# Attention with its projections in a block's first step, and a new order of the work behind it

## The chip, the cores and the metric

The kernel runs on one core of a Trainium2 chip. The metric is the device time of one execution in microseconds (us). Engines are named as in the profile: PE (TensorE, matmuls), ACT (ScalarE), DVE (VectorE), POOL (GpSimd) and SP (the queue that issues DMAs).

## The reference

Four layers follow one another on an fp32 tensor of 16 x 384 x 16 x 16 (two clips of 8 frames, 2048 tokens a clip):

```python
# layer 0: attention over all tokens of a clip, 12 heads of 32
qk = (xt @ qk_w.T).reshape(B, N, 2, nh, HEAD_DIM)
...
attn = softmax(einsum('bhnd,bhmd->bhnm', q * scale, k), axis=-1)
attn = alpha * eye + beta * attn - gamma * Cm          # Cm = 1/N everywhere
out = einsum('bhnm,bhmd->bhnd', attn, v)               # v is x itself
# layer 1: depthwise 7x7, LayerNorm, MLP 384->1536->384 with GELU and GRN, + residual
# layer 2: Sobel x and y, 768->384 fusion, LayerNorm, GELU, + residual
# layer 3: BN, 1x1, depthwise 3x3, BN, 1x1, + residual; linear attention over 8 heads, 1x1;
#          LayerNorm, MLP 384->1536->384 with GELU, + residual
```

With `alpha`, `beta` and `gamma` each a number per head, the result of layer 0 is `alpha * x + beta * softmax(qk) x - gamma * mean(x)`: the means over a clip's tokens enter as a bias.

## The kernel before

**Attention.** A *unit* is one clip `b` and one group `g` of four heads (128 channels): 6 units. A unit has 4 *blocks* `n` of 512 queries, and a block has 16 *steps* `t` of 128 keys, so there are 24 blocks and 384 steps. In a step `scores` (L465) does the four heads' score matmuls into two PSUM tiles `st` and two exponentials on ACT into `e`; `weighted` (L483) does the four heads' matmuls of values into the accumulator `av`, and DVE adds the exponentials into `s`. The main loop (L596 to L606) calls `scores` of a step, then `weighted` of the step before, so `weighted` lags one step behind. `av` and `dn` (the denominators) have one PSUM bank each; `st` has three tiles of two banks.

The exponentials' sums become denominators by a matmul with ones (`weights`, L526). `ADDS` (L56) says for each block how many steps DVE sums before such a matmul: with 16, one matmul group at the block's end; with 8, two; with 4, four. Groups inside a block are cut into four parts of 128 queries and spread over later steps.

At a block's last step (L517 to L524) ACT copies `av` to `va` and makes `xg = alpha * x + gm`, where `gm` holds the means; two steps later `finish` copies the denominators to `r` (ACT), and step by step follow a logarithm and an exponential of its negative on ACT (`log`, `invert`: the reciprocal) and four DVE operations (`defect`, `refine`, `scale`, `put`). `due` is the list of such deferred pieces, by step number.

Queries and keys of the next blocks are projected in pairs (`project`, L578) into one `st` tile: 6 matmuls of 128x128x512, each in two passes, and then two ACT copies. This happens in step `SLOT` = 5 of a block (L603), in all blocks up to the first two of the last unit. A key's projection also issues the load of its 512 values by SP. The clip means (L574 to L577) are DVE reductions for the first clip, in steps 0 to 12, and for the second clip 12 ACT accumulations of a chunk each and a closing DVE pair, in every second step from 156 on.

**Filling.** `fill` (L1505), called after each step, gives DVE's spare time to the next layer: the depthwise 7x7 of layer 1 (`conv`, 48 multiply-adds a channel chunk) from step `FIRST` on, and the first layer-1 blocks up to their MLP (`leads`) from step `LEAD` = 326. How much is spare comes from `pace` (L196): an estimate of PE's and DVE's time for each step.

**Later work.** After attention, `plan.all` (L1584) orders the operations of all remaining tasks by a list scheduler: among the operations that could start within `SLACK` of the earliest it takes that of the lowest rank. Ranks per task are in `RANK` (L46): `mid` (layer 2 and most of layer 3), `l1` (layer 1), `l3c` (the last MLP), `conv`. The two MLPs of 8 image blocks run in the groups of `TURNS` (L36), as weights are loaded for a group. The order is fixed when the kernel is built: each engine keeps program order (`InOrder`, L88).

Of the kernel before, what the change touches and what calls it, by code (L numbers as in the profile page):

```python
# [9 lines left out]
F32 = mybir.dt.float32  # L10
# [5 lines left out]
P = 128  # L16
# [12 lines left out]
NBLK = N // BLK  # L29
NIP = NBLK  # L30
NQC = N // P
SLOT = 5
LEAD = 20 * NQC + 6
FIRST = NQC + 10

TURNS = (  # L36
    (0, ((0, 0), (0, 1), (0, 2), (0, 3),)),
# [6 lines left out]
AFTER = ('x4', 0, 2)  # L44

RANK = {  # L46
    "mid": ((7.3, 48.9, 70.4, 82.6), (148.1, 31.6, -5.4, 26.9)),
    "l1": ((125.5, 116.9, 31.6, 62.9), (92.4, 221.3, 38.4, 14.0)),
    "l3c": ((153.2, 335.5, -64.8, 29.8), (10.7, 30.4, 62.7, 79.9)),
    "conv": 470.9,  # L50
}
SLACK = 0.1944
LOGEXP = "natural_log_exp_and_others"
JUNK = 2

ADDS = (16, 16, 16, 16, 8, 16, 8, 4, 4, 16, 16, 16, 8, 8, 4, 8, 16, 16, 8, 8, 4, 8, 4, 4)  # L56
XB, YB, SB = 12, 4, 23
NLEAD = 2
TB = BLK // P
RB = 2 * HW  # L60
HD3 = 48
MOST, LEAST, TINY = 1e18, 1e-11, 1e-19
# [133 lines left out]
def pace(t):  # L196


    n, i = divmod(t - 1, NQC)
    adds = ADDS[n]  # L200
    pe, dve = 2.066, 2.275 if t and i % adds else 0.0
    at = i - adds - 1
    parts = sum(j * adds // 4 == at % adds for j in range(4)) if at >= 0 else 0
    if parts:
        pe += 0.22 * parts
    elif i == 1 and n > 0:
        pe += 0.87
    else:
        pe += 0.09
    if n > 0:  # L210
        dve += {5: 0.66, 6: 0.66, 7: 0.6, 8: 0.66}.get(i, 0.0)
    return pe, dve


# [185 lines left out]
def attention(tc, X, xt, L0, block, small, col, cols, ones, load_qk, banks, fill, bound, tiny):  # L400
# [6 lines left out]
    with ExitStack() as actx:  # L407
# [45 lines left out]
            return made, early, late  # L453


        due = {}

        def unit(u, made, gm):

# [23 lines left out]
            def weighted(n, t, es):  # L483
                if t == 0:
                    acc["av"] = pacc.tile([P, BLK], F32, tag="av", name=f"av_{u}_{n}")
                for h in range(4):
                    pe.matmul(
                        acc["av"][HD * h : HD * (h + 1), :],
                        v[t // TB][:, (t % TB) * P + HD * h : (t % TB) * P + HD * (h + 1)],
                        es[h // 2][:, h % 2, :],  # L490
                        start=(t == 0),
                        stop=(t == NQC - 1),
                    )
                at = t % adds[n]
                for i in range(2):
                    if at == 0:
                        sums[i] = es[i]
                    elif at == 1:
                        s = sp.tile([P, 2, BLK], F32, tag="s", name=f"s_{u}_{n}_{t}_{i}")
                        dve.tensor_tensor(s, sums[i], es[i], ALU.add)  # L500
                        sums[i] = s
                    else:
                        dve.tensor_tensor(sums[i], sums[i], es[i], ALU.add)


                k = (u * NBLK + n) * NQC + t
                if at == adds[n] - 1:
                    parts = 1 if t == NQC - 1 else 4
                    for i in range(parts):
                        due.setdefault(k + 2 + i * adds[n] // 4, []).append(  # L510
                            lambda i=i, summed=dict(sums): weights(
                                n, t, summed, ts(i, BLK // parts)
                            )
                        )
                for f in due.pop(k, ()):
                    f()
                if t == NQC - 1:  # L517
                    va = op.tile([P, BLK], F32, tag="va", name=f"va_{u}_{n}")
                    act.activation(va, acc["av"], AF.Copy, scale=1.0)
                    xg = op.tile([P, BLK], F32, tag="xg", name=f"xg_{u}_{n}")  # L520
                    act.activation(
                        xg, X[b][n][:, g, :], AF.Identity, scale=col("alpha", g), bias=gm
                    )
                    due[k + 2].append(lambda: finish(n, va, xg))  # L524

            def weights(n, t, summed, at):  # L526
                if t == adds[n] - 1 and at.start == 0:
# [7 lines left out]
                        stop=(t == NQC - 1),  # L535
                    )

            def finish(n, va, xg):

                if g == 0:  # L540
                    L0[b][n] = block(f"l0_{b}_{n}")
                k = u * NBLK + n
                r = op.tile([P, BLK], F32, tag="r", name=f"r_{u}_{n}", bufs=1)
                w = op.tile([P, BLK], F32, tag="w", name=f"w_{u}_{n}", bufs=1)
                act.activation(r, acc["dn"], AF.Identity, accum_out=bound[:, 0, k : k + 1])
# [18 lines left out]
                def put():  # L564
                    dve.scalar_tensor_tensor(
                        L0[b][n][:, g, :], va, col("beta", g), xg, ALU.mult, ALU.add
                    )

                for i, f in enumerate([log, invert, defect, refine, scale, put]):
                    due.setdefault((k + 1) * NQC + 3 + i, []).append(f)  # L570

            return scores, weighted

        means = [channel_means(dve, op, X, cols, b, act if b else None) for b in range(NB)]  # L574
        for b, (_, steps) in enumerate(means):
            for i, s in enumerate(steps):
                due[b * NC * NBLK * NQC - 36 * b + (3 - b) * i] = [s]  # L577
        def project(name, steps):  # L578
            pp = bank2(name)
            for copy in [f(pp[:, i, :]) for i, f in enumerate(steps)]:  # L580
                copy()
            return 2.7 * len(steps)

        made, early, late_steps = projections(*units[0])
# [5 lines left out]
        for u, (b, g) in enumerate(units):  # L590
            steps = late_steps
            scores, weighted = unit(u, made, means[b][0][:, g : g + 1])
            if u + 1 < len(units):
                made, early, late_steps = projections(*units[u + 1])
                steps = steps + early
            for n in range(NBLK):  # L596
                for t in range(NQC):
                    es = scores(n, t)
                    added = 0.0
                    if before:  # L600
                        before()
                    before = lambda f=weighted, a=(n, t, es): f(*a)
                    if t == SLOT and steps:  # L603
                        added = project(f"p_{u}_{n}", steps[:2])
                        del steps[:2]
                    fill((u * NBLK + n) * NQC + t, added)  # L606
            assert not steps
        before()
        while due:
            for f in due.pop(min(due)):  # L610
                f()
# [4 lines left out]
def conv_seq_kernel(  # L616
# [391 lines left out]
                yield from extra(f, h)  # L1008
        return hid, made

    def second(hid, first, name, ready, last, before=None):

        po = []
        for f in range(NFC):
# [1 line left out]
            after = [ready[f]] if before is None else [(yield from before(f))]  # L1016
            m = tensor(
                NC * BLK,
                after=after + [("wb", first, k)],
                takes=[("mm", NC)] if f == 0 else [],  # L1020
                gives=[("s", 1)] + ([("wb", 1)] if last and f % NG == NG - 1 else []),
            )
# [13 lines left out]
    def layer1(b, i):  # L1036

        n = f"l1_{b}_{i}"
        at, before, last = turns[b, i, 0]
# [5 lines left out]
        gx = pools["tiny"].tile([P, 2, NFC], F32, tag="gx", name=f"gx_{n}")  # L1045
        squares = []

        def norms(f, h):
# [17 lines left out]
        gs = pools["tiny"].tile([P, 2], F32, tag="gs", name=f"gs_{n}")  # L1066
        dve.tensor_reduce(gs, gx, AX.X, ALU.add)
        m = tensor(120, after=[a], takes=[("mm", 1)])
        yield m
# [4 lines left out]
        gm = pools["tiny"].tile([P, 2], F32, tag="gmean", name=f"gmean_{n}")  # L1074
        dve.tensor_scalar(gm, pg[:, :2], 1.0 / FF, 1e-6, ALU.mult, ALU.add)
        dve.reciprocal(gm, gm)
        for k in range(2):
# [21 lines left out]
                )  # L1099
            return a  # L1100

        po, m = yield from second(hid, at, n, None, last, normed)
# [342 lines left out]
    def layer3c(b, i):  # L1445
# [7 lines left out]
        at, before, last = turns[b, i, 1]  # L1453
        hid, made = yield from hidden(
            d, at, "L3_mlp_b1", n, ds, before, ("hid", b, i, 1), last
        )
        po, m = yield from second(hid, at, n, made, last)
        for c in range(NC):
            a = fused(
                BLK,  # L1460
# [14 lines left out]
    turns, before = {}, None  # L1475
    for at, (k, group) in enumerate(TURNS):
        for b, i in group:
            turns[b, i, k] = (at, before, (b, i) == group[-1])
            before = ("hid", b, i, k)

    bias = Task("bias", 0, fusion_bias())
# [17 lines left out]
    if fast:  # L1499
# [5 lines left out]
        def fill(t, added=0.0):  # L1505
# [3 lines left out]
            if t < 0:  # L1509
                while plan.step(bias):  # L1510
                    pass
                return
            if t % NQC == 10 and t > NQC:
                u, i = divmod(t // NQC - 1, NBLK)
                plan.mark(("l0", u // NC, i, u % NC))
            length, work = pace(t)
# [161 lines left out]
```

## Time and profile before

| | us |
|---|---|
| median of 3 runs | 2658.97 (2658.66 to 2663.05) |
| the profiled execution | 2660.87 |
| its span, first to last instruction | 2659.1 |
| attention, first scores to last denominators | 19.3 to 1030.0 |
| first block, from its first value matmul to the next block's | 24.60 to 66.24 |
| a block with 16 steps a sum (the sixth) | 232.75 to 274.18 |
| a block with 8 (the seventh) | 274.18 to 316.14 |
| a block with 4 (the fifteenth) | 612.60 to 655.38 |
| longest PE gap | 6.54, at 1063.1 |
| PE's last matmul ends | 2652.5 |

All instructions of the program stand under line 98, that of the helper that records them, so groups are told apart by their tiles: `e<-st` is an exponential, `av<-e,v` a value matmul. A timeline line gives the start, the time that a run of equal instructions takes, the engine, the operation, shapes and count, and in brackets the idle time ahead of it with what ended it.

### The profile page before, as it was taken

How to read it: one execution, taken by the hardware profiler on the slowest of the kernel's cores; microseconds unless marked ns; L12 is line 12 of the kernel's file. 1: busy time of each engine (PE TensorE's matmuls, PEld its weight loads, DVE VectorE, ACT ScalarE, POOL GpSimd, SP SyncE). 2: the span in 40 equal slices, each digit the busy share in tenths (PEclk: the TensorE clock that was granted, in tenths of full speed). 3: DMA queues.
4: the chain of work that ended last, by engine and by line, in shares of the span. 5: the costliest groups of instructions: out<-in, count | busy, mean ns of one | idle time of the engine just before them, and what ended most of it. 6: DMA issues, size and time to landing. Idle time of an engine off the chain costs nothing. (4 is left out here: it accounts for less than half of the span.)

```text
span 2659.1 us, 30865 instructions
## 1 busy us (share of the span) xinstructions
PE 2623.8 (99%) x12005; PEld 1035.7 (39%) x12005; DVE 2028.8 (76%) x2604; ACT 1573.3 (59%) x2339; POOL 7.5 (0%) x54
## 2 busy tenths in 40 slices
PE   9999999999999999899999999999999999999999
PEld 2222232223222323344444544444444444445443
DVE  5999999999999989999999999999462140542300
ACT  6888888988888887454636534455246551415311
POOL 0000000000000000000000000000000000000000
PEclk9999999999999999899999999999999999999999
DMA  4000000000000003000001101101210000000000
GB/s 155 1 13 5 5 11 3 13 5 5 9 1 1 13 1 131 0 0 1 0 1 36 36 0 48 37 11 48 71 36 12 24 24 12 13 12 1 0 21 16
DMA packets 29275, 55.56 MB, mean 21 GB/s; under 512 B 1728, under 2 KB 14400, under 8 KB 29120
## 3 DMA queue, kind: packets, MB, share of 16 engines
q1 hardware_dynamic: 29120, 53.51, 6.0%
q8 instruction: 96, 1.57, 0.2%
q14 instruction: 59, 0.48, 0.1%
HBM read 47.21 MB, written 6.29 MB: 20 GB/s over the span
## 5 line engine op out<-in xcount | busy, mean ns | idle before, releaser
L98 ACT ACTIVATE e<-st 128x1024 f32<-128x1024 f32 x768 | 742.1, 1025 | 77.2 <-PE st L98 64.0
L98 DVE TENSOR_TENSOR s<-s,e 128x1024 f32<-128x1024 f32 x568 | 657.5, 1219 | 18.3 <-ACT e L98 17.4
L98 DVE SCALAR_TENSOR_TENSOR y<-l,vec,y 128x420 f32<-128x420 f32 (+8 forms) x1152 | 654.7, 636 | 3.6 <-ACT y L98 0.7
L98 PE MATMUL st<-q,k 32*128 32x512 f32 x3072 | 481.7, 641 | 2.9 <-ACT e L98 1.5
L98 PE MATMUL av<-e,v 128*32 128x512 f32 x3072 | 410.6, 605 | 6.1 <-ACT va L98 3.7
L98 PE MATMUL po_l<-hid_l,wb 128*128 128x512 f32 x576 | 259.7, 600 | 4.0 <-ACT hid_l L98 4.0
L98 PE MATMUL ph_l3c<-d_l3c,wa 128*128 128x512 f32 x576 | 259.1, 594 | 0.0
L98 PE MATMUL ph_l<-y,wa 128*128 128x512 f32 x576 | 258.6, 594 | 0.0
L98 PEld LDWEIGHTS st<-q,k 32*128 32x128 f32 x3072 | 152.0, 183 | 270.6 <-issue 145.7
L98 PE MATMUL po_l3c<-hid_l3c,wb 128*128 128x512 f32 x576 | 253.7, 593 | 0.0
L98 ACT ACTIVATE hid_l3c<-ph_l3c,vec 128x512 f32<-128x512 f32 x96 | 65.8, 687 | 264.8 <-PE ph_l3c L98 264.2
L98 PEld LDWEIGHTS av<-e,v 128*32 128x32 f32 x3072 | 60.6, 108 | 299.9 <-issue 273.0
L98 DVE SCALAR_TENSOR_TENSOR o_l3c<-po_l3c,vec,l 128x512 f32<-128x512 f32 x24 | 17.8, 749 | 197.7 <-PE po_l3c L98 196.6
L98 PEld LDWEIGHTS po_l<-hid_l,wb 128*128 128x128 f32 x576 | 109.4, 192 | 139.7 <-issue 127.6
L98 PEld LDWEIGHTS po_l3c<-hid_l3c,wb 128*128 128x128 f32 x576 | 109.0, 190 | 137.2 <-issue 136.2
L98 PEld LDWEIGHTS ph_l3c<-d_l3c,wa 128*128 128x128 f32 x576 | 108.7, 190 | 137.0 <-issue 130.7
L98 PEld LDWEIGHTS ph_l<-y,wa 128*128 128x128 f32 x576 | 108.5, 190 | 136.2 <-issue 126.1
L98 ACT ACTIVATE hid_l<-ph_l,vec 128x512 f32<-128x512 f32 x96 | 65.8, 686 | 135.1 <-PE ph_l L98 134.8
L98 DVE TENSOR_TENSOR s<-e,e 128x1024 f32<-128x1024 f32 x100 | 117.8, 1220 | 30.7 <-ACT e L98 26.1
L98 PE MATMUL p<-x,wqk_sb 128*128 128x512 f32 x288 | 131.8, 608 | 4.1 <-DMA x<-in_x_dram 4.1
L98 DVE SCALAR_TENSOR_TENSOR g_l3a<-h_l3a,dw,g_l3a 128x450 f32<-128x450 f32 (+1 forms) x192 | 119.2, 699 | 14.9 <-ACT g_l3a L98 14.7
L98 ACT ACT_TABLE_LOAD x88 | 112.9, 1283 | 16.7 <-PE ph_l L98 9.4
(153 smaller groups left out, 2285.8 us busy)
## 6 DMA issues: line engine op xcount, KB each, us to landing
wa<-in_w_dram SPq DMA_DIRECT2D x9, 768.0 KB, 4.3
wb<-in_w_dram SPq DMA_DIRECT2D x9, 768.0 KB, 4.8
wa<-in_mlp_w_dram SPq DMA_DIRECT2D x9, 768.0 KB, 4.3
wb<-in_mlp_w_dram SPq DMA_DIRECT2D x9, 768.0 KB, 4.4
v<-in_xt_dram SPq DMA_DIRECT2D x24, 256.0 KB, 2.7
out_dram<-o_l3c SPq DMA_DIRECT2D x24, 256.0 KB, 2.0
x<-in_x_dram SPq DMA_DIRECT2D x7, 768.0 KB, 11.0
qkv<-in_qkv_wT_dram SPq DMA_DIRECT2D x3, 576.0 KB, 11.5
```

What stands on the lines that cost most here:

```text
L98: self.last = self.tc.keep_in_program_order(make(*args, **kw))
```

## The change

- Projections move from step 5 to step 0 of a block, behind `scores` of that step and `weighted` of the last step of the block before.
- The copies `va` and `xg` of the block before come in that step too (`finish` now returns them as `copies`), ahead of the projection's matmuls; behind them one chunk of the second clip's means in each of blocks 1 to 12 (two pieces in the last of these).
- The last denominator matmul, `r`, logarithm, inversion and the DVE operations come in steps 1, 1, 2, 3, 4, 5, 6, 7 (before: 1, 1, 3, 4, 5, 6, 7, 8). Parts of denominator matmuls stay within their block.
- `ADDS` changes for three blocks: 3 (16 to 8), 13 (8 to 16), 23 (4 to 16).
- `pace` gets other rates; `FIRST` is one step earlier, as is the step in which a block of layer 0 counts as done (9 instead of 10).
- `RANK` and `SLACK` are new. In the later work a second MLP layer may start only when that of the block before it in its group is planned; three small tiles get 4 buffers instead of 2.

```diff
-SLOT = 5
-FIRST = NQC + 10
+FIRST = NQC + 9
...
-    "mid": ((7.3, 48.9, 70.4, 82.6), (148.1, 31.6, -5.4, 26.9)),
-    "l1": ((125.5, 116.9, 31.6, 62.9), (92.4, 221.3, 38.4, 14.0)),
-    "l3c": ((153.2, 335.5, -64.8, 29.8), (10.7, 30.4, 62.7, 79.9)),
-    "conv": 470.9,
+    "mid": ((-26.8, 59.3, 121.4, 6.1), (-9.9, 89.9, 76.1, -44.6)),
+    "l1": ((99.2, -11.0, 54.4, 108.8), (48.0, 102.3, -47.4, 64.0)),
+    "l3c": ((77.2, 238.7, 72.9, 521.4), (108.5, 22.1, 82.6, 122.3)),
+    "conv": 381.3,
 }
-SLACK = 0.1944
+SLACK = 0.1686
...
-ADDS = (16, 16, 16, 16, 8, 16, 8, 4, 4, 16, 16, 16, 8, 8, 4, 8, 16, 16, 8, 8, 4, 8, 4, 4)
+ADDS = (16, 16, 16, 8, 8, 16, 8, 4, 4, 16, 16, 16, 8, 16, 4, 8, 16, 16, 8, 8, 4, 8, 4, 16)
...
-    pe, dve = 2.066, 2.275 if t and i % adds else 0.0
+    pe, dve = 2.156, ADD if t and i % adds else 0.0
     at = i - adds - 1
-    parts = sum(j * adds // 4 == at % adds for j in range(4)) if at >= 0 else 0
-    if parts:
-        pe += 0.22 * parts
-    elif i == 1 and n > 0:
-        pe += 0.87
-    else:
-        pe += 0.09
+    if at >= 0:
+        pe += 0.22 * sum(j * adds // 4 == at % adds for j in range(4))
+        pe += 0.22 * (adds < 8 and i == NQC - 1)
     if n > 0:
-        dve += {5: 0.66, 6: 0.66, 7: 0.6, 8: 0.66}.get(i, 0.0)
+        pe += 0.87 * (i == 1)
+        dve += {4: 0.66, 5: 0.66, 6: 0.6, 7: 0.66}.get(i, 0.0)
...
-                if at == adds[n] - 1:
-                    parts = 1 if t == NQC - 1 else 4
-                    for i in range(parts):
-                        due.setdefault(k + 2 + i * adds[n] // 4, []).append(
-                            lambda i=i, summed=dict(sums): weights(
-                                n, t, summed, ts(i, BLK // parts)
-                            )
+                if t == NQC - 1:
+                    ends.append(finish(n, dict(sums)))
+                elif at == adds[n] - 1:
+                    for i in range(4):
+                        due.setdefault(min(k + 2 + i * adds[n] // 4, k - t + NQC - 1), []).append(
+                            lambda i=i, summed=dict(sums): weights(n, t, summed, ts(i, P))
                         )
...
-                if t == NQC - 1:
-                    va = op.tile([P, BLK], F32, tag="va", name=f"va_{u}_{n}")
-                    act.activation(va, acc["av"], AF.Copy, scale=1.0)
-                    xg = op.tile([P, BLK], F32, tag="xg", name=f"xg_{u}_{n}")
-                    act.activation(
-                        xg, X[b][n][:, g, :], AF.Identity, scale=col("alpha", g), bias=gm
-                    )
-                    due[k + 2].append(lambda: finish(n, va, xg))
...
-                for i, f in enumerate([log, invert, defect, refine, scale, put]):
-                    due.setdefault((k + 1) * NQC + 3 + i, []).append(f)
+                todo = [sum_up, sums_out, log, invert, defect, refine, scale, put]
+                for i, f in zip((1, 1, 2, 3, 4, 5, 6, 7), todo):
+                    due.setdefault((k + 1) * NQC + i, []).append(f)
+                return copies
...
-        for b, (_, steps) in enumerate(means):
-            for i, s in enumerate(steps):
-                due[b * NC * NBLK * NQC - 36 * b + (3 - b) * i] = [s]
+        for i, s in enumerate(means[0][1]):
+            due[3 * i] = [s]
+        later = list(means[1][1])
...
-                    if t == SLOT and steps:
+                    if t == 0 and ends:
+                        ends.pop()()
+                        for f in later[: 1 + (len(later) == 2)]:
+                            f()
+                            later.remove(f)
+                    if t == 0 and steps:
                         added = project(f"p_{u}_{n}", steps[:2])
                         del steps[:2]
...
-                after=after + [("wb", first, k)],
+                after=after + [("wb", first, k)] + ([turn] if f == 0 and turn else []),
+                makes=done if f == NFC - 1 else None,
...
-            if t % NQC == 10 and t > NQC:
+            if t % NQC == 9 and t > NQC:
```

`project` itself now emits each of its two steps' matmuls and copy in turn:

```diff
-            for copy in [f(pp[:, i, :]) for i, f in enumerate(steps)]:
-                copy()
+            for i, f in enumerate(steps):
+                f(pp[:, i, :])()
```

More of the change, by code (lines that the diff above doesn't have):

```diff
@@ L59 @@
 TB = BLK // P
+ADD = 2.275
 RB = 2 * HW
@@ L453, in projections @@
             return made, early, late
-        due = {}
+        due, ends = {}, []
         def unit(u, made, gm):
@@ L536, in weights, with finish, copies, sum_up @@
                     )
-            def finish(n, va, xg):
-                if g == 0:
-                    L0[b][n] = block(f"l0_{b}_{n}")
+            def finish(n, summed):
                 k = u * NBLK + n
+                va = op.tile([P, BLK], F32, tag="va", name=f"va_{u}_{n}")
+                xg = op.tile([P, BLK], F32, tag="xg", name=f"xg_{u}_{n}")
                 r = op.tile([P, BLK], F32, tag="r", name=f"r_{u}_{n}", bufs=1)
                 w = op.tile([P, BLK], F32, tag="w", name=f"w_{u}_{n}", bufs=1)
-                act.activation(r, acc["dn"], AF.Identity, accum_out=bound[:, 0, k : k + 1])
+                def copies():
+                    act.activation(va, acc["av"], AF.Copy, scale=1.0)
+                    act.activation(
+                        xg, X[b][n][:, g, :], AF.Identity, scale=col("alpha", g), bias=gm
+                    )
+                def sum_up():
+                    weights(n, NQC - 1, summed, ts(0, BLK))
+                def sums_out():
+                    act.activation(
+                        r, acc["dn"], AF.Identity, accum_out=bound[:, 0, k : k + 1]
+                    )
                 def log():
@@ L564, in put @@
                 def put():
+                    if g == 0:
+                        L0[b][n] = block(f"l0_{b}_{n}")
                     dve.scalar_tensor_tensor(
@@ L608, in attention @@
         before()
+        ends.pop()()
         while due:
@@ L1009, in hidden, with second @@
         return hid, made
-    def second(hid, first, name, ready, last, before=None):
+    def second(hid, first, name, ready, last, before=None, turn=None, done=None):
         po = []
@@ L1038, in layer1 @@
         n = f"l1_{b}_{i}"
-        at, before, last = turns[b, i, 0]
+        at, before, former, last = turns[b, i, 0]
         s, a = yield from centred_later(n, b, i)
@@ L1043, in layer1 @@
         ds = yield from affine(y, "L1_ln_g", "L1_ln_b", a)
-        gx = pools["tiny"].tile([P, 2, NFC], F32, tag="gx", name=f"gx_{n}")
+        gx = pools["tiny"].tile([P, 2, NFC], F32, tag="gx", name=f"gx_{n}", bufs=4)
         squares = []
@@ L1065, in layer1 @@
         yield a
-        gs = pools["tiny"].tile([P, 2], F32, tag="gs", name=f"gs_{n}")
+        gs = pools["tiny"].tile([P, 2], F32, tag="gs", name=f"gs_{n}", bufs=4)
         dve.tensor_reduce(gs, gx, AX.X, ALU.add)
@@ L1073, in layer1 @@
         yield ready
-        gm = pools["tiny"].tile([P, 2], F32, tag="gmean", name=f"gmean_{n}")
+        gm = pools["tiny"].tile([P, 2], F32, tag="gmean", name=f"gmean_{n}", bufs=4)
         dve.tensor_scalar(gm, pg[:, :2], 1.0 / FF, 1e-6, ALU.mult, ALU.add)
@@ L1100, in normed @@
             return a
-        po, m = yield from second(hid, at, n, None, last, normed)
+        po, m = yield from second(
+            hid, at, n, None, last, normed, former, ("sec", b, i, 0)
+        )
         for c in range(NC):
@@ L1452, in layer3c @@
         ds = yield from affine(d, "L3_ln_w", "L3_ln_b", a)
-        at, before, last = turns[b, i, 1]
+        at, before, former, last = turns[b, i, 1]
         hid, made = yield from hidden(
@@ L1456, in layer3c @@
         )
-        po, m = yield from second(hid, at, n, made, last)
+        po, m = yield from second(
+            hid, at, n, made, last, None, former, ("sec", b, i, 1)
+        )
         for c in range(NC):
@@ L1477, in conv_seq_kernel @@
         for b, i in group:
-            turns[b, i, k] = (at, before, (b, i) == group[-1])
+            former = None if (b, i) == group[0] else ("sec", *before[1:])
+            turns[b, i, k] = (at, before, former, (b, i) == group[-1])
             before = ("hid", b, i, k)
```

## The prediction

> **What bounds the kernel now.** I read the page first, then the busy time by stretch, then the timelines of a block's edge.
>
> ```profile
> span 2659.1 us, 30865 instructions
> ## 1 busy us (share of the span) xinstructions
> PE 2623.8 (99%) x12005; PEld 1035.7 (39%) x12005; DVE 2028.8 (76%) x2604; ACT 1573.3 (59%) x2339; POOL 7.5 (0%) x54
> ```
>
> PE is busy nearly throughout. The stretches show that this holds in each stage, and who stands close behind (columns: length, then each engine's busy time):
>
> ```profile
> 25.00:1030.00 1005.00, 998.18 (x7415) 292.73 (x7407) 956.97 (x983) 844.42 (x1009) 0.00 (x0) 1.00 0.02 7
> 1030.00:1850.00 820.00, 804.42 (x2277) 368.13 (x2278) 800.39 (x1265) 422.93 (x823) 3.38 (x24) 0.99 0.08 27
> 1850.00:2659.00 809.00, 802.51 (x2267) 367.18 (x2266) 266.29 (x336) 296.35 (x495) 3.38 (x24) 1.00 0.06 21
> ```
>
> DVE follows PE closely in attention (to 1030 us) and in the first half of the later work; the last third is PE's alone. So time comes and goes with PE's gaps, with PE's work, and with stalls inside its "busy" time. In quiet stretches two attention steps take 4.31 us (scores start at 263.98 and 268.29), 2.155 a step, while ACT needs 2 x 0.92 for its exponentials. ACT has 0.3 us a step to spare, and a longer insert reaches PE within a step.
>
> A block's edge, ACT then PE, and below them the first projection of all:
>
> ```profile
> 273.52 0.60 ACT L98 ACTIVATE va<-av 128x512 f32<-128x512 f32 x1
> 274.00 0.82 ACT L98 ACTIVATE xg<-x,gm,vec 128x512 f32<-128x512 f32 x1
> 274.70 3.77 ACT L98 ACTIVATE e<-st 128x1024 f32<-128x1024 f32 x4
> ...
> 290.52 0.59 ACT L98 COPY q<-p 128x512 f32<-128x512 f32 x1 [3.60 <-PE p L98]
> ```
>
> ```profile
> 274.18 1.07 PE L98 MATMUL av<-e,v 128*32 128x512 f32 x8 [0.28 <-ACT va L98]
> 275.17 1.74 PE L98 MATMUL st<-q,k 32*128 32x512 f32 x8
> ...
> 285.07 5.42 PE L98 MATMUL p<-x,wqk_sb 128*128 128x512 f32 x12
> ```
>
> ```profile
> 11.43 0.59 ACT L98 COPY k<-p 128x512 f32<-128x512 f32 x1 [0.48 <-PE p L98]
> ```
>
> Copies va and xg hold ACT 1.18 us (273.52 to 274.70), and PE waits openly and stretches its next scores. The projection keeps PE 5.35 us (285.07 to 290.42); ACT idles 3.60 of it. The third thing to see: the copy of q waits until 290.52, the end of all 12 matmul passes, though q's own six (0.43 apart) end at 287.9. At 11.43 it is the same: ACT had been free since 10.95 and k's matmuls were over at 9.1. The two halves of the projection's PSUM tile are guarded as one.
>
> **The change, part by part.** *The projection's own order.* Before, all 12 passes went out ahead of both copies. Now the first copy is issued between the halves. If the tile is guarded as one for a write after a read too, the second half's matmuls must wait for the first copy: 0.04 us to its start (290.487 to 290.525), 0.59 for it, some 0.10 back to PE: 0.73 us of an idle PE. Where a mean stands on ACT, it is more: ACT gets to the copy at 1.18 (scores to exponential) + 1.84 (two of them) + 1.18 (va, xg) + 0.83 = 5.03 us after the step's scores start, the first half is done at 1.08 + 1.0 + 2.6 = 4.68, so 0.32 more, 1.05. Blocks 1 to 12 have a mean, 13 to 20 none, block 21 projects one half only: 12 x 1.05 + 8 x 0.73 = 18.4 us. If the halves are guarded apart it is nothing. No row shows a write after a read; the nearest rows, the copies' starts, say one guard, so I take +18.4. Behind the waiting matmuls stand the next scores and all of PE; nothing covers it.
>
> *The edge.* A block with 16 steps a sum runs from 232.75 to 274.18 (first value matmuls): 41.43 us. Less 16 x 2.155 = 34.48, the projection 5.35 and the denominators' matmuls 0.87, 0.73 remain for the edge, and this goes under the projection. But the logarithm (0.61, 283.77 to 284.38) and the inversion (0.75 with its accumulator read), today just ahead of and inside ACT's 3.60 idle us, fall into plain steps 3 and 4. The last block, without a projection, shows their price: its step with the logarithm takes 2.44 instead of 2.07, the one with the inversion about 0.15 more; by arithmetic the latter could cost 0.35. So -0.73 + 0.52 to 0.72: -0.1 for each of 9 projecting 16-step blocks. Blocks with 8 steps a sum take 41.96 (274.18 to 316.14); less four partial sums of 0.22 as well, 0.38 remain, so they save 0.38 and pay 0.52 to 0.72: +0.25 for each of 8. Those with 4 take 42.78 (612.60 to 655.38), their 12 partial sums fill the slack, and 0.3 at most can be saved: +0.3 for each of 4. Sum -0.9 + 2.0 + 1.2 = +2.3 us; with both pieces free it would be 9 x -0.73 - 8 x 0.38 - 4 x 0.3 = -10.8, at the dearest +5.
>
> *The start.* Here nothing covers a wait:
>
> ```profile
> 24.60 1.63 PE L98 MATMUL av<-e,v 128*32 128x512 f32 x8 [1.96 <-DMA v<-in_xt_dram]
> 26.16 2.09 PE L98 MATMUL st<-q,k 32*128 32x512 f32 x8
> 28.18 1.14 PE L98 MATMUL av<-e,v 128*32 128x512 f32 x8
> ```
>
> Scores start at 19.27, the second value group at 28.18, and a projection follows: 33.53. With it right after the first scores the second value group starts at 19.27 + 1.08 + 5.35 + 1.08 + 2.1 = 28.9: -4.6 us, with 1.96 of DMA wait and 1.4 of half clock (0.5 for 3.4 us from 25.0) in it. One guard takes this back: the first copy comes when ACT's table is loaded, 10.95, so the second half runs from 11.6 to 14.2 instead of to 11.39 (+2.8), the next pair loses 0.73, the moved one 0.73: -0.3 in all. The Trainium skill (TensorE: Matmul & The Clock Gate, "Why this matters for your kernels") lets the clock fall only after idle gaps over about 3 us; by it the 1.96 us gap is not the cause and the 1.4 may stay. By the trace the drop stands right behind that gap, while gaps of 0.8 and 1.21 (907.5, 963.3) left the clock at 1.0; so I price the new gaps of 0.73 and 1.05 without a drop.
>
> *The means.* Twelve ACT accumulations between steps of blocks 9 to 11 (41.63, 42.39 and 41.79 us, 1.55 above 3 x 41.42) go: -1.5.
>
> *Sum groups.* Block 3 goes from 16 to 8 (+0.54 by the blocks' lengths), 13 back (-0.54), the last from 4 to 16 (-1.36): -1.4. DVE gets 6 adds more, 6 x 1.135 = 6.8 us, and by the filler's new rates 2.7 us more of conv; DVE was busy 39.9 of 41.4 us in a 16-step block, so PE hides them: 0. Without that cover, up to 9.5 us.
>
> *DMAs.* The moved steps issue v loads five steps earlier on a quiet SP queue, into slots long free: 0.
>
> *Later work.* The same matmuls in another order; the new condition on second MLP layers binds the planner alone. PE's gaps there are some 6 us in crumbs and one transition:
>
> ```profile
> 1069.62 0.59 PE L98 MATMUL pg_l<-gs_l,ones 128*128 128x2 f32 x2 [6.54 <-DVE gs_l L98]
> 1073.81 8.75 PE L98 MATMUL po_l<-hid_l,wb 128*128 128x512 f32 x13 [3.60 <-ACT hid_l L98]
> ```
>
> With the clock at 0.5 until 1079.7 behind it (3 us lost) that is 13 us. The reduction gs ran 3.1 us after its input was ready (1066.3 to 1069.39), behind conv taps. The new order could win up to 10 us or add a second such transition, +13; conv is about as far along, so I take 0.
>
> The sum: 18.4 + 2.3 - 0.3 - 1.5 - 1.4 = +17.5 us on the profiled execution's 2660.9 (span 2659.1 and 1.8 around it): 2678.4. The median shown is 1.9 lower: **2676.5**.
>
> **The rivals.** *Halves guarded apart (A, faster).* For: a first-layer matmul starts at 1405.79 while ACT still writes another third of its SBUF input, so SBUF is guarded by region; against: both copies above. Then 2.3 - 4.6 - 1.5 - 1.4 = -5.2: 2654; with logarithm and inversion free as well, -18: 2641. It decides if the first copy starts inside the projection and PE doesn't pause. *Apart, and nothing gained (C).* The exposed pieces at +5, the slow clock staying (-3.2 for the start): -1: 2658. *The new order starves PE (D).* DVE, 800 of 820 us busy after attention, brings the second image block late, and a second gap like that of 1063 comes on top: 2676.5 + 13 = 2690. For: PE waits on gs there already; against: DVE idles 630 us in all.
>
> **How the numbers follow.** This kernel's measurement can tell 0.2%, 5.3 us, from no change. Forecast 0.62, D 0.11, A 0.18, C 0.09. Forecast and D are slower: 0.72 (a hundredth left for a lucky order). A is faster by hardly 5.3 to 18: 0.17. The rest, C and what lies between: 0.11. The range reaches from half way into A, 2652, to 2688, short of D.
>
> **What would show it.** Right: 23 pauses of 0.7 to 1.1 us on PE inside projections, ended by ACT's copy of q or k; the longest in blocks 1 to 12; scores first at about 22.8; no wait for va in blocks 1 to 21; steps 3 and 4 at 2.2 to 2.6; attention ending near 1047. Wrong: 12 passes in a row as before (A, C), or gaps after 1060 beyond 13 us (D).

## The result, and the profile after

| | before | after |
|---|---|---|
| median | 2658.85 us (2658.66 to 2663.05) | 2685.48 us (2685.38 to 2685.68) |
| profiled execution | 2660.87 | 2685.38 |
| its span | 2659.1 | 2683.6 |

The ratio of the mean times is 1.0096, with a 95% interval of 1.0079 to 1.0114: the change makes the kernel about 1% slower. The forecast was 2676.5, in a range of 2652 to 2688. The sign and its cause are as forecast; the loss is 9 us larger.

From the page of the changed kernel, its head and the group of the projection's matmuls (out<-in, count, then busy time and mean ns of one, then the idle time ahead of the group and what ended most of it):

```profile
span 2683.6 us, 30716 instructions
## 1 busy us (share of the span) xinstructions
PE 2634.2 (98%) x11909; PEld 1039.8 (39%) x11909; DVE 2033.4 (76%) x2610; ACT 1561.6 (58%) x2326; POOL 7.4 (0%) x54
...
L98 PE MATMUL p<-x,wqk_sb 128*128 128x512 f32 x288 | 140.0, 624 | 22.2 <-ACT q L98 10.8
```

Before, the same group had only the wait for the first DMA ahead of it:

```profile
L98 PE MATMUL p<-x,wqk_sb 128*128 128x512 f32 x288 | 131.8, 608 | 4.1 <-DMA x<-in_x_dram 4.1
```

Now 18 us of idle time stand ahead of them, ended by ACT's copies of q and k, and 8 us more are inside their "busy" time.

The busy time by stretch, cut where the first MLP matmul starts (1056.3) and 820 us later (length, then PE, PEld, DVE, ACT, POOL, the granted clock, the DMA share and GB/s):

```profile
30.00:1056.00 1026.00, 1006.22 (x7319) 294.86 (x7318) 963.63 (x989) 850.77 (x1010) 0.00 (x0) 1.00 0.02 6
1056.00:1876.00 820.00, 804.21 (x2281) 368.81 (x2280) 802.63 (x1279) 420.96 (x823) 3.31 (x24) 0.99 0.08 27
1876.00:2684.00 808.00, 801.45 (x2266) 367.46 (x2264) 263.64 (x324) 281.35 (x482) 3.38 (x24) 1.00 0.06 21
```

The two later stretches are what they were. All of the loss is ahead of them. In the first stretch PE is idle for 20 us of 1026; before, it was idle for 7 of 1005.

One moved projection, on PE and below it on ACT (start, time of the run, engine, operation, count, and in brackets the idle time ahead and what ended it):

```profile
322.25 0.40 PE L98 MATMUL dn<-s,ones 128*32 128x128 f32 x8
322.58 2.84 PE L98 MATMUL p<-x,wqk_sb 128*128 128x512 f32 x6
326.10 2.84 PE L98 MATMUL p<-x,wqk_sb 128*128 128x512 f32 x6 [0.68 <-ACT k L98]
328.87 1.14 PE L98 MATMUL st<-q,k 32*128 32x512 f32 x8
```

```profile
323.12 0.60 ACT L98 ACTIVATE va<-av 128x512 f32<-128x512 f32 x1
323.60 0.82 ACT L98 ACTIVATE xg<-x,gm,vec 128x512 f32<-128x512 f32 x1
324.30 0.64 ACT L98 ACTIVATE mean<-x 128x512 f32<-128x512 f32 x1
324.82 0.21 ACT L98 ACTIVATION_READ_ACCUMULATOR mean<-x 128x1 f32 x1
325.46 0.59 ACT L98 COPY k<-p 128x512 f32<-128x512 f32 x1 [0.43 <-PE p L98]
```

The second six matmuls start when the copy of the first half is over (325.46 + 0.59 = 326.05), although they write the other half of the tile. From 322.58 to 328.87 the pair takes 6.29 us; 12 in a row took 5.35 before (285.07 to 290.42). So a pair costs 0.94: 0.68 of open pause, and 0.26 by which two runs of six (2 x 2.84) are longer than one run of 12 (5.42), which shows as busy. The mean of x fits in ahead of the copy, and ACT still waits 0.43 us for PE.

In the profiled execution the 24.5 us of span come about so, by the starts of the same matmuls in both traces. Only the 33.53 is reckoned: before, the first block's projection comes later (at 35.72), so its 5.35 are added to the second value group's 28.18, as in the prediction.

| stretch | before | after | difference |
|---|---|---|---|
| to the second value group and projection | 33.53 | 35.38 | +1.85 |
| from there to the last block's first value group | 957.85 | 979.88 | +22.03 |
| the last block, to the first MLP matmul | 38.5 | 41.0 | +2.5 |
| later work, to PE's end | 1622.6 | 1621.2 | -1.4 |
| behind PE's end | 6.6 | 6.15 | -0.45 |

The start, on PE:

```profile
4.30 5.06 PE L98 MATMUL p<-x,wqk_sb 128*128 128x512 f32 x6 [4.30 <-DMA x<-in_x_dram]
11.35 4.54 PE L98 MATMUL p<-x,wqk_sb 128*128 128x512 f32 x6 [1.99 <-ACT k L98]
...
19.36 5.42 PE L98 MATMUL p<-x,wqk_sb 128*128 128x512 f32 x12 [0.68 <-ACT k L98]
24.71 1.14 PE L98 MATMUL st<-q,k 32*128 32x512 f32 x8
25.78 2.84 PE L98 MATMUL p<-x,wqk_sb 128*128 128x512 f32 x6
29.30 2.84 PE L98 MATMUL p<-x,wqk_sb 128*128 128x512 f32 x6 [0.68 <-ACT q L98]
```

Three pairs pause here, and the first scores come at 24.71 instead of 19.27. The wait for v is gone as foreseen, but the first pair's pause is 1.99 us, since ACT loads its table until 10.70 and copies k only then, and six matmuls behind it take 4.54 us instead of 2.84. The granted clock (the column before the DMA share) says why:

```profile
6.00:12.20 6.20, 4.21 (x7) 1.66 (x7) 1.24 (x11) 3.64 (x5) 0.00 (x0) 1.00 1.00 401
12.20:15.60 3.40, 3.40 (x5) 1.33 (x4) 0.00 (x0) 0.00 (x0) 0.00 (x0) 0.50 1.03 415
15.60:24.60 9.00, 8.32 (x21) 3.38 (x19) 2.03 (x3) 1.75 (x3) 0.00 (x0) 1.00 1.02 417
```

The end of attention, PE, then DVE:

```profile
1049.11 2.98 PE L98 MATMUL av<-e,v 128*32 128x512 f32 x16
1054.14 2.19 PE L98 MATMUL dn<-s,ones 128*32 128x512 f32 x8 [2.04 <-DVE s L98]
```

```profile
1036.97 18.25 DVE L98 TENSOR_TENSOR s<-s,e 128x1024 f32<-128x1024 f32 x16
```

The last block now sums 16 steps on DVE, whose adds run on until 1055. PE has nothing else to do and waits for them (the bracket of 2.04).

### The profile page after: what moved, and what is told of

Read it like the earlier page. It is cut to its first block, busy times and chain, and to the rows that moved or that the text cites. A ratio compares the mean times of both kernels' runs of the same rounds, so it can differ in the third digit from the quotient of the medians.

```text
span 2683.6 us, 30716 instructions
## 1 busy us (share of the span) xinstructions
PE 2634.2 (98%) x11909; PEld 1039.8 (39%) x11909; DVE 2033.4 (76%) x2610; ACT 1561.6 (58%) x2326; POOL 7.4 (0%) x54
## 3 DMA queue, kind: packets, MB, share of 16 engines
HBM read 47.21 MB, written 6.29 MB: 20 GB/s over the span
## 5 line engine op out<-in xcount | busy, mean ns | idle before, releaser
L98 DVE TENSOR_TENSOR s<-s,e 128x1024 f32<-128x1024 f32 x580 | 671.3, 1217 | 6.8 <-ACT e L98 5.5
L98 PE MATMUL st<-q,k 32*128 32x512 f32 x3072 | 488.6, 641 | 3.1 <-ACT e L98 2.5
L98 PEld LDWEIGHTS st<-q,k 32*128 32x128 f32 x3072 | 159.5, 183 | 285.8 <-issue 170.5
L98 PE MATMUL p<-x,wqk_sb 128*128 128x512 f32 x288 | 140.0, 624 | 22.2 <-ACT q L98 10.8
L98 DVE TENSOR_TENSOR s<-e,e 128x1024 f32<-128x1024 f32 x94 | 110.7, 1218 | 53.4 <-ACT e L98 52.2
L98 ACT ACTIVATE hid_l<-hid_l,vec,gx_l 128x256 f32<-128x256 f32 x192 | 103.3, 613 | 20.1 <-DVE gx_l L98 20.1
```

The costliest lines, as they stand in the source:

```text
L98: self.last = self.tc.keep_in_program_order(make(*args, **kw))
```

## The experiments

The theory: the loss is the copy between the halves, which PE must wait for because the two halves lie in one PSUM tile; the rest of the change is worth little. The rivals: the move of the projection to the block's edge costs by itself, the new order of the later work does, or the loss has nothing to do with the tile.

**Copies behind both halves (e1_copies_last).** The changed kernel with the projection's own order as before:

```diff
-            for i, f in enumerate(steps):
-                f(pp[:, i, :])()
+            for copy in [f(pp[:, i, :]) for i, f in enumerate(steps)]:
+                copy()
```

> The changed kernel with one thing undone: both halves' matmuls of a projection are issued ahead of both copies, as before. Theory (the copy between the halves makes PE wait, 0.68 us open and 0.26 us to get going again in each of 21 pairs, 19.7 us, and 5.4 us ahead of the first scores): the pauses go, a projection takes 5.35 us again, the first scores start at 19.3; 2685.5 - 25 = 2660.5, between 2658 and 2663. Rival 1 (the exposed logarithm and inversion and the fuller DVE are what costs, and a pause only takes the place of another wait): above 2675. Rival 2 (the new order of the later work costs it): above 2680.

Measured: 2660.1 us (2659.42 to 2661.94), beside 2659.27 for the kernel before; ratio 1.0004, 0.9995 to 1.0014. The span is 2658.0. A projection is 12 matmuls in a row again:

```profile
311.65 5.42 PE L98 MATMUL p<-x,wqk_sb 128*128 128x512 f32 x12
317.00 1.14 PE L98 MATMUL st<-q,k 32*128 32x512 f32 x8
```

The first scores come at 20.37, and the first MLP matmul at 1031.1. The first scores had been expected at 19.3: the program's first 12 matmuls take 8.43 us here and 7.26 in the kernel before; in the experiment with the means below, whose start is the same code as here, they take 7.41. So this differs between executions. The whole loss is gone with these two lines, and all the rest of the change together gives neither a gain nor a loss that the interval can tell.

**The opposite swap in the kernel before (e2_before_copy_between).** The same two lines, the other way round:

```diff
-            for copy in [f(pp[:, i, :]) for i, f in enumerate(steps)]:
-                copy()
+            for i, f in enumerate(steps):
+                f(pp[:, i, :])()
```

> The kernel before with this one thing done: each half's copy right behind its matmuls, the projection still in step 5. Theory: a pause of 0.68 us in each of 21 pairs, 21 x 0.94 = 19.7 us, and the first scores 5.4 us later, of which the 1.96 us wait for v and 1.4 us of half clock are taken back: +21.7, so 2680.5, between 2677 and 2684. Rivals 1 and 2: 2658 to 2664.

Measured: 2681.9 us (2681.14 to 2682.72); ratio 1.0086, 1.0069 to 1.0103. Its projections on PE, in step 5 as before:

```profile
291.20 2.84 PE L98 MATMUL p<-x,wqk_sb 128*128 128x512 f32 x6
294.71 2.84 PE L98 MATMUL p<-x,wqk_sb 128*128 128x512 f32 x6 [0.68 <-ACT q L98]
```

The same 0.68 with no va, xg or mean near by. The span is 2679.3, 20.2 us longer than before's, with no other part of the change in it. The pause is the same in step 5 as in step 0, so the place in the block plays no part in it.

**A tile for each half (e3_two_tiles).** The changed kernel with its copies between the halves, and each half in its own PSUM tile:

```diff
-            pp = bank2(name)
             for i, f in enumerate(steps):
-                f(pp[:, i, :])()
+                f(bank2(f"{name}_{i}")[:, 0, :])()
```

> The changed kernel with the copy still issued between the halves, but each half in a PSUM tile of its own. Theory (the two halves of one tile are guarded as one, so the second half's first matmul waits for the reader of the first): no pause, the first copy runs during the second half; 2657 to 2663. If it is the order of issue itself that makes PE wait, whatever the tile: pauses stay, 2683 to 2688. If the extra tile costs the scores theirs: step 2 behind a projection longer than 2.3 us, and 2663 to 2675.

Measured: 2660.53 us (2659.69 to 2662.2); ratio 1.0004, 0.9994 to 1.0013. PE, then ACT:

```profile
312.19 5.42 PE L98 MATMUL p<-x,wqk_sb 128*128 128x512 f32 x12
317.54 1.14 PE L98 MATMUL st<-q,k 32*128 32x512 f32 x8
```

```profile
315.07 0.59 ACT L98 COPY k<-p 128x512 f32<-128x512 f32 x1 [0.43 <-PE p L98]
317.64 0.59 ACT L98 COPY k<-p 128x512 f32<-128x512 f32 x1 [1.99 <-PE p L98]
```

The first copy now runs at 315.07 while PE goes on with the second half. So it isn't the order of issue that makes PE wait, it is that both halves stand in one tile. Yet the time is that of the first experiment: the early copy by itself gains nothing. PE does its 12 matmuls in a row either way, and starts the next scores at 317.54, ahead of the second copy (317.64), so they don't wait for it.

**The new order of the later work alone (e4_before_new_order).** The kernel before with the new `RANK`, `SLACK`, the turn of second MLP layers and the buffers:

```diff
...
-    "conv": 470.9,
+    "conv": 381.3,
 }
-SLACK = 0.1944
+SLACK = 0.1686
...
-        po, m = yield from second(hid, at, n, None, last, normed)
+        po, m = yield from second(hid, at, n, None, last, normed, former, ("sec", b, i, 0))
```

> The kernel before with only the new ranks, slack, condition and buffers of the later work; attention as before. Theory (the order is worth nothing either way: from the first MLP matmul to the last, 1622.6 us before and 1621.2 after): 2656 to 2663. Rival 2 (the order is what lost, hidden by something else in the changed kernel): above 2668.

Measured: 2660.58 us (2659.31 to 2662.86); ratio 1.0004, 0.9994 to 1.0014. Its later work takes 1622.5 us to PE's end, before's 1622.6: the order is worth nothing by itself.

**One half at step 0, one at step 3 (e5_halves).** On top of the first experiment, an attempt at something better: the logarithm and the inversion cost PE time in steps 3 and 4, and a half of the projection would cover them.

```diff
-                for i, f in zip((1, 1, 2, 3, 4, 5, 6, 7), todo):
+                for i, f in zip((1, 1, 2, 2, 4, 5, 6, 7), todo):
...
-                    if t == 0 and steps:
-                        added = project(f"p_{u}_{n}", steps[:2])
-                        del steps[:2]
+                    if t in (0, 3) and steps:
+                        added = project(f"p_{u}_{n}_{t}", steps[:1])
+                        del steps[:1]
```

> From e1: a projection in two single halves, one in step 0 and one in step 3 of a block, and the inversion right behind the logarithm, both ahead of step 3's half on ACT. Theory (under the old place the two pieces were covered, in steps 3 and 4 they cost 0.37 us each, which eats what the edge gains): steps 3 and 4 at 2.07 to 2.24 without their projection, some 0.7 us less in each of 20 blocks, less 0.2 for a second change to projections: -10 to -14, so 2646 to 2650. Rival (the edge's copies weren't free either, or the second half brings its own stall): 2655 or more.

Measured: 2648.72 us (2647.67 to 2650.52), beside 2660.34; ratio 0.9958, 0.9942 to 0.9975. It is faster than both kernels. PE, then ACT, at a block's edge:

```profile
308.11 2.84 PE L98 MATMUL p<-x,wqk_sb 128*128 128x512 f32 x6
310.88 1.14 PE L98 MATMUL st<-q,k 32*128 32x512 f32 x8
...
318.11 2.84 PE L98 MATMUL p<-x,wqk_sb 128*128 128x512 f32 x6
320.88 1.14 PE L98 MATMUL st<-q,k 32*128 32x512 f32 x8
```

```profile
319.04 0.72 ACT L98 ACTIVATE w<-r,tiny 128x512 f32<-128x512 f32 x1
319.79 0.63 ACT L98 ACTIVATE w<-w 128x512 f32<-128x512 f32 x1
320.33 0.19 ACT L98 ACTIVATION_READ_ACCUMULATOR w<-w 128x1 f32 x1
320.99 0.59 ACT L98 COPY k<-p 128x512 f32<-128x512 f32 x1 [0.47 <-PE p L98]
```

The logarithm and the inversion lie under the second half, and the two steps behind it are back at 2.07 and 2.24. A block with 16 steps a sum takes 40.67 us, against 41.21 in the first experiment and 41.43 before.

**Four steps a sum in the last block (e6_halves_last4, e7_last4).** The wait for DVE at the end of attention should go if the last block sums 4 steps again, on top of the halves and on top of the first experiment:

```diff
-ADDS = (16, 16, 16, 8, 8, 16, 8, 4, 4, 16, 16, 16, 8, 16, 4, 8, 16, 16, 8, 8, 4, 8, 4, 16)
+ADDS = (16, 16, 16, 8, 8, 16, 8, 4, 4, 16, 16, 16, 8, 16, 4, 8, 16, 16, 8, 8, 4, 8, 4, 4)
```

> e5 with the last block's sums over 4 steps again, as before the change. Theory (with 16 the last block of attention waits for DVE's adds, 2.04 us open, and takes 41.0 us instead of 38.5): attention ends 2 to 4 us earlier and DVE gets 6.8 us of conv more: 2 to 4 us below e5. If the rival holds that fewer denominator matmuls are worth it: 1 to 2 us above e5.

> e1 with the last block's sums over 4 steps again. Theory: 2.5 us less in the last block, 2656 to 2659 beside e1's 2660. The prediction's term (-1.4 us from 16 steps) being right: 2661 to 2662.

Measured: 2695.02 (2693.54 to 2696.16, ratio 1.0132, 1.0116 to 1.0149) and 2731.19 (2729.73 to 2731.92, ratio 1.0266, 1.0249 to 1.0284). Both expectations missed. The first MLP matmul of the first of these does come 2.1 us earlier (1017.31 instead of 1019.40), but its later work takes 1669.3 us, 47 more; that of the second takes 1692.9, 72 more. In the second the first MLP matmul comes no earlier (1031.04 instead of 1031.10): the last block is 1.3 us shorter (39.70 instead of 41.00), but block 22 ahead of it takes 1.6 more at half the clock, as told in the last section. The second one, by stretch, then its largest gap on PE and what DVE did in it:

```profile
1031.00:1850.00 819.00, 760.23 (x2152) 347.78 (x2151) 797.28 (x1283) 417.84 (x771) 3.41 (x24) 0.96 0.07 24
1850.00:2724.00 874.00, 859.40 (x2395) 391.31 (x2393) 264.09 (x310) 304.15 (x550) 3.40 (x24) 0.99 0.07 21
```

```profile
1354.41 2.74 PE L98 MATMUL pc_l3a<-l,ca 128*128 128x512 f32 x6
1373.28 5.07 PE L98 MATMUL pd_l3a<-g_l3a,cb 128*128 128x512 f32 x6 [16.14 <-DVE g_l3a L98]
```

```profile
1359.52 14.81 DVE L98 SCALAR_TENSOR_TENSOR g_l3a<-h_l3a,dw,g_l3a 128x450 f32<-128x450 f32 x24
```

`ADDS` also feeds the planner: with fewer adds it reckons with more conv done by the end of attention, and orders the later work differently. DVE is as busy as ever (797 of 819 us), but the matmul that is next in PE's order needs the 24 multiply-adds of a depthwise convolution in layer 3, and PE waits 16 us for them.

**The same with the plan kept (e9_last4_plan_kept).** The halves, 4 steps a sum in the last block, and a planner that still reckons with 16:

```diff
+PLANNED = (16, 16, 16, 8, 8, 16, 8, 4, 4, 16, 16, 16, 8, 16, 4, 8, 16, 16, 8, 8, 4, 8, 4, 16)
+ADDS = PLANNED[:-1] + (4,)
...
-    adds = ADDS[n]
+    adds = PLANNED[n]
```

> e5 with the last block's sums over 4 steps, but the filler's estimate still made for 16 there, so that it gives conv the same share and the planner of the later work starts from the same state as in e5. Theory (e6 and e7 lost 47 and 72 us in the later work because ranks that were found for one state of conv make a bad order from another; the shorter sums themselves are good): the later work back to 1620 to 1624 us, attention ending 2 us earlier than e5's 1019.4, 2645 to 2648. Rival (the shorter sums themselves harm the later work, by the denominators' end or the conv behind it): 2680 or more.

Measured: 2648.55 us (2646.95 to 2649.37), beside 2658.71; ratio 0.9961, 0.9947 to 0.9975. The first MLP matmul comes at 1017.72, 1.7 earlier than with 16 steps a sum, and the later work takes 1622.9. So the shorter sums had not been the harm, it was what the planner made of them. What they gain themselves, about 1 us of span (2647.6 to 2646.7), is less than the interval can tell.

**The means back between the steps (e8_means_in_steps).** The first experiment, with the means of both clips where the kernel before has them:

```diff
-        for i, s in enumerate(means[0][1]):
-            due[3 * i] = [s]
-        later = list(means[1][1])
+        for b, (_, steps) in enumerate(means):
+            for i, s in enumerate(steps):
+                due[b * NC * NBLK * NQC - 36 * b + (3 - b) * i] = [s]
...
-                        for f in later[: 1 + (len(later) == 2)]:
-                            f()
-                            later.remove(f)
```

> e1 with the second clip's means back between steps of blocks 9 to 11. Theory (between steps they cost 1.55 us in all, under the projection nothing): blocks 9 to 11 longer by 1.5 us in all, 2661 to 2662.5. If the means cost nothing where they were: 2660, blocks 9 to 11 as in e1.

Measured: 2663.2 us (2662.07 to 2664.53), beside 2660.34; ratio 1.0011, 1.0001 to 1.002. Blocks 9 to 11 (counted from 0) take 41.48, 42.43 and 44.45 us instead of 41.27, 41.21 and 42.62: 3.26 more, where about 1.5 were expected. In block 11 a mean meets the logarithm, which no longer lies under a projection, and two pieces of the next layer; steps 3 and 4 go to 4.80 and 3.31 (3.84 and 2.44 in the first experiment). PE there, and the granted clock of the stretch behind its gap (the column before the DMA share):

```profile
498.48 1.47 PE L98 MATMUL st<-q,k 32*128 32x512 f32 x4 [1.27 <-ACT e L98]
...
499.10:502.50 3.40, 3.40 (x16) 0.72 (x16) 3.37 (x6) 2.68 (x5) 0.00 (x0) 0.50 0.00 0
```

So one stretch of half clock, worth 1.4 to 1.7 us by those of the last section, is part of the 3.26. By this estimate 1.6 to 1.9 are left for the means themselves, about what was expected. Block 22 takes 1.6 us more besides (43.91 instead of 42.27), again at half clock, and against it the first value group comes 1.1 us earlier, at a start whose code is the same. In all it is 2 us (2.9 above the kernel before here, 0.8 in the first experiment), which the intervals hardly tell from nothing.

## Why the prediction was right, and where it was short

**The guard: right.** From two copies that came late in the trace of before, the prediction read one guard for the whole PSUM tile, and from that a wait which this trace didn't contain. All 23 pauses that the prediction counted are there, one of 1.99 us and 22 of 0.67 or 0.68. (A small misreading did no harm: k's matmuls at the start of the trace of before were over at 8.81, not 9.1.) Of the other signs, the pauses in blocks 1 to 12 are not longer than the rest, the first scores come at 24.71 instead of 22.8, and attention ends at 1056 instead of 1047. The swap of two lines makes the loss or takes it away in either kernel, and a tile for each half takes it away too. The Trainium skill (PSUM — Partial Sum Buffer, "PSUM bank collisions raise a hardware error") wants engines kept apart by bank and quadrant, and reports that accesses to different banks run clean. Its "Specifications (TRN2)" give a bank 2 KiB, so each half here (512 elements of 4 bytes) should be a bank of its own, an estimate from that figure, and the wait wasn't one the chip needs. That the two-tile kernel copies one half at 315.07 while PE writes the other until 317.5 agrees with it; a copy beside matmuls into the other half of the same tile was not run.

**The price of a pair: two errors that cancel.** The prediction took 0.73 for a plain pair and 1.05 for one with a mean. Every pair costs 0.94. The 0.26 of a second run of six was left out. And the mean's 0.32 never came: ACT was reckoned to be done with the mean 5.03 us after the start of the step's scores, PE with the first half after 4.68. In the trace ACT is done after 4.91 (5.06 in block 1), and PE only after 4.95 to 5.35, as its six matmuls take 2.84 and not 2.6, and in some blocks denominator matmuls come ahead of them. In the block shown ACT is through at 325.03 and waits 0.43 us. That the two errors cancel is luck: 20 x 0.94 = 18.8 instead of 18.4.

**The start: mis-sized, -0.3 reckoned, +1.85 measured.** The pieces were the right ones: the pauses, and no wait for v. But the first pair's pause of 1.99 us was reckoned as a delay alone. The prediction priced "the new gaps of 0.73 and 1.05 without a drop" of the clock, and put no drop behind this longest one, though it had itself read a drop behind the 1.96 of before. The half clock from 12.2 to 15.6 makes six matmuls 1.7 us longer (4.54 instead of 2.84), and the two shorter pauses cost 0.94 instead of 0.73 each: together 2.1 of the 2.15 that were missed. The old drop, behind the wait for v, went away, and a new one came in its place. In the second experiment the first pause was 2.12 us and no drop followed (six matmuls took 2.84), so part of this row is chance.

**The blocks' edge and the means: as reckoned in most blocks, +0.8 in all reckoned, +2.15 measured.** Without the 0.94, most projecting blocks take 41.22 (16 steps a sum), 42.14 (8) and 43.03 (4; blocks 8 and 14) instead of 41.43, 41.96 and 42.78: -0.21, +0.18 and +0.25, where -0.1, +0.25 and +0.3 stood. The logarithm's and the inversion's steps take 2.44 each, 4.88 for the two instead of 4.31; this 0.57 is inside the 0.52 to 0.72 given. What was missed is the other work on ACT that now meets these two exposed pieces: step 3 takes 3.14 in block 7 and 3.84 in blocks 11 and 20 (before, pieces of that kind stood in plain steps of 3.23 and 3.18, in blocks 12 and 20), and steps 3 and 4 of block 21 some 2.95 each. With its copies last the changed kernel is still 2.15 us longer than before in this part (30.09 to 990.1, 960.0 against 957.85), where edge and means had been +0.8 together. In the changed kernel block 22 adds another 1.6 (43.9 instead of 42.27), a half clock from 988.4 to 991.8.

**The last block: the wrong sign, -1.36 reckoned, +2.5 measured.** "Sum groups" let the last block go from 4 steps a sum to 16 at a gain, by the lengths of blocks that have a successor. There DVE's adds run on under the next block. The last one has none, and PE waits 2.04 us for them. The prediction's "so PE hides them: 0" holds for every block but the one in which PE runs out of work. Setting it back alone shortens the last block by 1.3 us with the copies last (e7) and by 1.7 with the halves (e9, 39.83 instead of 41.49). The rest, some 1 us, no run sets apart; the likely place are its steps 3 to 5 (3.14, 3.13 and 2.53), in which pieces of the next layer stand on ACT beside the logarithm and the inversion.

**Later work: right.** Reckoned 0, measured -1.4 of 1622.6 in the changed kernel and -0.1 with the order alone. The rival in which the new order starves PE did not occur; the one long transition of PE is where it was, 39.7 us behind the first MLP matmul:

```profile
1095.95 0.59 PE L98 MATMUL pg_l<-gs_l,ones 128*128 128x2 f32 x2 [6.52 <-DVE gs_l L98]
1100.20 6.22 PE L98 MATMUL po_l<-hid_l,wb 128*128 128x512 f32 x9 [3.67 <-ACT hid_l L98]
```

That such a rival is real, the kernel with four steps a sum in the last block (e7) shows: PE is idle for 73 us of its later work, and for 22 before. The ranks hold for the state that they were found for.

**The median.** 2 us of the 9 are none of the kernel's: the profiled execution of before was 2.0 above its median, and the prediction took that off, while that of after was on its median. The other 7 are the start (2.15), the stretch of the blocks (22.03 instead of 18.4 + 0.8, so 2.8), the last block (3.9), and -1.85 for the later work and what lies behind it.

## What to carry to other kernels

A PSUM tile of several parts may be guarded as one: before a read is put between two writes to parts of one tile, look in the trace whether a reader of one part has ever started while another part was being written, and give each part its own tile if not. A piece that looks free under a long matmul run is free only there; a move has to be priced at the place where it lands, with all the other pieces that land in the same steps, and at the end of a stage, where no next block covers an engine that runs behind. A planner's constants go with the state they were tuned for: a gain of 1 us in one stage cost 47 to 72 in the next, until the planner's input was held fixed.

## What the runs showed of the hardware that was not expected

Gaps of 1.15 to 2 us on PE can already halve TensorE's granted clock, and whether they do depends on where they lie. In each trace all changes of the granted clock stand on a grid of 3.413 us (after: 12.2 and 988.4, 286 periods of it), and the half clock lasts whole periods: 3.4, 6.8, 10.2, 13.7 or 17.1 us, but for the last one, which the end of the trace cuts. In block 22 every kernel that ran has a gap of 1.15 to 1.21 us on PE, which ACT's exponential ends. In eight of the eleven (after, e2, e4 and e5 to e9) it lies whole inside one period of the grid, and the clock is at 0.5 for the next one. In the other three (before, e1, e3) a boundary cuts it, 0.4 and 0.8 in before, and the clock stays at 1.0. The gap and the stretch behind it, in the changed kernel and then in the first experiment:

```profile
987.10 1.13 PE L98 MATMUL st<-q,k 32*128 32x512 f32 x4 [1.21 <-ACT e L98]
988.40:991.80 3.40, 3.40 (x24) 0.95 (x16) 3.40 (x4) 1.40 (x2) 0.00 (x0) 0.50 0.02 5
...
963.59 1.13 PE L98 MATMUL st<-q,k 32*128 32x512 f32 x4 [1.21 <-ACT e L98]
965.90:969.30 3.40, 3.40 (x40) 1.08 (x40) 3.40 (x5) 2.32 (x3) 0.00 (x0) 1.00 0.02 5
```

Three more gaps agree: the 1.27 of e8's block 11, the 1.99 at the start of after and the 1.96 of before lie inside one period and bring the drop. The 2.12 of e2 is cut into 0.27 and 1.85 and doesn't. So the length alone does not decide, and not all is settled by this: a gap of 1.46 at 23.3 in e4, inside a period, left the clock at 1.0, as did gaps of 1.0 and 1.1 and all the pauses of 0.68. What sets these apart from the 1.15, no run here shows.

The Trainium skill (TensorE: Matmul & The Clock Gate, "What's actually happening") describes this window: 3413 ns, running freely, its place against the kernel a matter of chance. The grid agrees with it. The advice in that page's "Why this matters for your kernels", no gaps over about 3 us, was not enough here: gaps of a third of a period brought the drop.

The price is 1.4 to 1.7 us for one period at half clock: 1.4 in block 22 of e2 and e4 beside before, 1.6 in after, e7 and e8 beside e1, 1.7 at the start of after. So the 1.6 us in block 22 come or go with the place of the grid, with no change of the code there.
